# Cross-attention with a mixture of experts: transposes placed behind the bias, results read in five groups, scatters that leave out empty rows

## The chip, the cores and the metric

The kernel runs on one core of a Trainium2 chip. The metric is the device time of one execution in microseconds (us), the median of several runs. TensorE (PE in the profile, PEld its weight loads), VectorE (DVE), ScalarE (ACT), GpSimd (POOL) and SyncE (SP) run side by side and wait for one another by semaphores. SP, ACT and POOL issue the transfers (DMA).

## What is computed

All arrays are float32. `x` is (4, 512, 512), the context (4, 1024, 512).

```python
def attention(query, kv):                       # 16 heads of 32
    q, gate = query @ Wq.T, sigmoid(query @ Wg.T + bg)
    k, v = split(kv @ Wkv.T, 2)
    q, k = f(q), f(k)                           # f(x) = x + 1 if x > 0 else exp(x), per head
    z = 1 / (q . k.sum(tokens) + 1e-6)
    return (q @ (k.T @ v) * z * gate) @ Wo.T

def experts(x):                                 # 8 experts, each token goes to its best 2
    w, sel = top_k(x @ Wr, 2); w = softmax(w)
    return sum over the 2 choices of w * (x @ We[sel] + be[sel])

x = x + attention(layernorm(x), context)
x = x + experts(layernorm(x))
```

The two choices of a token are computed apart: 4 x 512 tokens make 4,096 rows that go through an expert.

## The kernel before

**Order of the work.** The four batches go through attention one after the other. After the attention of batch b, `choose` (L466) makes the normalized rows and picks two experts for each token, and `dispatch` (L514) works out by counting (small matmuls on ones) at which place of its expert's list each choice stands, and scatters the rows into `stream`, an array in DRAM with a region for each expert. A row carries two more numbers: where its result belongs (`home`), and its first expert.

**Expert tiles.** A tile is 128 rows of one expert's region. How many rows an expert has is known only on the chip, so lists of tiles are computed there: `tiles_of` (L582) counts tiles, `spans` (L593) orders them by groups and experts, `listed` (L614) writes for each tile the row at which it begins, and its expert. There are two lists. The early list (17 tiles, `EARLY`) is made when batch 3's attention is under way, from tiles that batches 0 to 2 have filled; it has three groups. The late list (up to 22 tiles, `LATE`; 18 of them, `SURE`, are always worked on, the rest stand behind a branch) is made after the dispatch of batch 3, from all that is left; its four groups are ordered so that the first tiles complete the results of batch 1, then 2, then the first half of 3, then the rest. Its wide operations on VectorE have 22 tiles x 4 groups x 8 experts = 704 columns.

**A step.** `run` (L671) is a generator that works through a list. For tile j, `rows` (L675) issues five loads on SP: four quarters of the rows, in 128-byte pieces, and a small one, `of`, with the two extra numbers. `turned` (L709) transposes the rows on VectorE in 32x32 blocks (L715) and computes the target row of each result from `of`: L724 makes `at` (home plus 1 if this is the token's second choice), L729 makes `to`, the smaller of `at` and `unread`. A row of `stream` without a token carries a home beyond every result; `unread` gives such a row a target of its own past the 4,096 results, so that it is written where nothing reads. `expert` (L735) does the matmuls with the expert's weights, adds the bias into `y` (L753) and lets GpSimd scatter `y` to the rows of `result` (L757). Step j loads tile j + 5, transposes tile j + 3, and then does the expert of tile j, whose bias is ordered behind that transpose; transposes and their small followers keep the order of the text. Early transposes go to four places in turn, so the transpose of tile j + 4 needs the matmuls of tile j to be done.

**Reading back.** The 16 token tiles (four a batch) each read their 256 rows of `result` (`fetch`, L810, 512 KB), add the two weighted results to the attention's output (`add`, L834, two VectorE operations), and store the tile (`store`, L849). `plan` and `begins` (L864 to L874) say at which step this is done: the reads of token tiles 0 to 3 at late steps -3 to 0 (negative steps are the last early ones), 4 to 7 at 5 to 8, 8 to 11 at 12 to 15, 12 and 13 at 16 and 17; adds three steps later, stores one after that. `also(j)` (L876) issues what is planned for step j, behind `y` of that step on VectorE and behind its scatter on GpSimd. What falls at step 18 or later comes after the loop, and there token tiles 14 and 15 are read by SP and ACT once all scatters have landed. A read waits for the scatters of as many tiles as `MOSTLY` says (13, 21, 29, 33 for the four batches). Whether that was enough is computed on the chip: `where_to_read` (L798) compares a group's last tile with the limit; if it was not, the read goes to rows of zeros at `NOWHERE`, and a branch at the end (L1020) reads everything again.

**Queues.** Scatters, reads and stores of the loop share GpSimd's queue, in the order of the text, each with a small memset (`mark`) ahead of it. SP issues the row loads. The order of the late list's instructions on VectorE among the steps is chosen when the program is built, mostly by the order of the text, and by when it is taken to be ready.

Of the kernel before, what the change touches and what calls it, by code (L numbers as in the profile page):

```python
# [9 lines left out]
F32 = mybir.dt.float32  # L10
I32 = mybir.dt.int32
# [6 lines left out]
P = 128  # L18
# [27 lines left out]
MOSTLY = (13, EARLY + 4, EARLY + 12, EARLY + 16)  # L46
NOWHERE = 2 * TOK + LATE * P
GROUPS = 4
# [3 lines left out]
def xattn_moe_kernel(  # L52
# [29 lines left out]

# [125 lines left out]
    unread = numbers("unread", [[P, LATE]], [P, LATE], base=2 * TOK, channel=1)  # L208
    expert_no = numbers("expert_no", [[0, GROUPS], [1, E]], [P, GROUPS, E])
    tile_no = numbers("tile_no", [[1, LATE]], [P, LATE])  # L210
# [303 lines left out]
    def dispatch(b):  # L514
# [21 lines left out]
        if b == B - 1:  # L536
            matmul(
                out=pp[:, NT + 1, :], lhsT=ones, rhs=acc[:, NT // 2, :], start=True, stop=True
            )
            counts["half"] = const.tile([P, E], F32, name="half")  # L540
            nc.vector.tensor_copy(counts["half"], pp[:, NT + 1, :])
# [72 lines left out]
    def listed(groups, n, name):  # L614
# [6 lines left out]
        def temp(what):  # L621
            t = work.tile([P, LATE * GROUPS * E], F32, tag="ex", name=what)
            return t[:, 0 : n * s].rearrange("p (n s) -> p n s", s=s)
# [47 lines left out]
    def run(lists, lo, n, early):  # L671
# [3 lines left out]
        def rows(j):  # L675


            row = nc.values_load(
                row_i[0:1, j : j + 1], [ET.SP], min_val=0, max_val=SLOTS,
                skip_runtime_bounds_check_because=why,  # L680
            )
            if j % 5 < 3:
                xg = cpool.tile([P, ROW], F32, tag="cT", name="xg")
            else:
                xg = kvpool.tile([P, ROW], F32, tag="v", name="xg", bufs=2)
            of = small.tile([P, 2], F32, tag="of", name="of", bufs=8)
            rows_of = stream[ds(row, P), :]
            parts = []
            for i in range(NC):
                parts.append(  # L690
                    (
                        xg[ts(i, HD), 0:D].rearrange("t (j f) -> t j f", j=NC),
                        rows_of[:, ts(i, P)].rearrange("(j t) f -> t j f", t=HD),
                    )
                )
            parts.append((of, rows_of[:, D:ROW]))
            for dst, src in parts:
                load = nc.sync.dma_start(out=dst, in_=src)  # L698
                latest["load"] = load
                if early:  # L700
                    behind(load, written["stream"][: 2 * NT * (B - 1)], "tokens of the tile")
                    early_loads.append(load)
                    for put in scatters.get(B - 1, []):
                        tc.declare_no_dep(load.ins, put.ins, reason=full_already)
                else:
                    behind(load, written["stream"], "tokens of the tile")
            return xg, of

        def turned(j, xg, of):  # L709
# [3 lines left out]
            else:  # L713
# [7 lines left out]
            at = small.tile([P, 1], F32, tag="at", name="at", bufs=8)  # L721
            tc.keep_in_program_order(latest["turn"])
            tc.keep_in_program_order(
                nc.vector.tensor_scalar(  # L724
                    at, of[:, 1:2], ranked[:, j : j + 1], of[:, 0:1],
                    ALU.is_equal, ALU.add,
                )
            )
            latest["turn"] = nc.vector.tensor_scalar(  # L729
                home_i, at, unread[:, j : j + 1], None, ALU.min  # L730
# [4 lines left out]
        def expert(j, xT, home_i):  # L735
# [15 lines left out]
            else:  # L751
# [9 lines left out]
                in_offset=None,  # L761
            )
            apart(put, "result", "each choice has a row; rows without a token go unread")
# [3 lines left out]

# [6 lines left out]
        def ahead(j):  # L774
            if j + 5 < n:
                with tc.issue_after(latest["load"].ins) if latest else nullcontext():
                    loaded.append(rows(j + 5))
            if j + 3 >= lo and loaded:
                ready.append(turned(j + 3, *loaded.pop(0)))

        for j in range(lo - 5, lo):
            ahead(j)
        yield
        for j in range(lo, n):
            ahead(j)
            with tc.issue_after(latest["turn"].ins):
                expert(j, *ready.pop(0))
            yield
# [3 lines left out]
    homes = [(wpool, "wq"), (wpool, "wg"), (wpool, "wo"), (big, "xT"), (big, "aT")]  # L792
    fetched = {}

    rows_of, spots = {}, {}
    soon = const.tile([P, B], F32, name="soon")

    def where_to_read(b, many, most):  # L798

        flag = soon[:, b : b + 1]  # L800
        nc.vector.tensor_scalar(flag, many, most, None, ALU.is_gt)
        spot = small.tile([P, 1], F32, tag="spot", name="spot")
        first_row = float(2 * L * b)
        nc.vector.tensor_scalar(
            spot, flag, float(NOWHERE) - first_row, first_row, ALU.mult, ALU.add
        )
        spots[b] = const.tile([P, 1], I32, name=f"spot_{b}")
        nc.vector.tensor_copy(spots[b], spot)

    def fetch(t, tiles, queue, sure=True):  # L810
# [5 lines left out]
        if sure:  # L816
            src = flat[:, t]
        else:
            b, o = t // NT, t % NT * 2 * P
            if b not in rows_of:  # L820
                rows_of[b] = nc.values_load(
                    spots[b][0:1, 0:1], [queue.engine], min_val=0, max_val=NOWHERE,
                    skip_runtime_bounds_check_because="one of two constants",
                )
            src = result[ds(rows_of[b] + o, 2 * P), :].rearrange("(p i) f -> p i f", i=2)
# [36 lines left out]
    half = B * NT - NT // 2  # L862
# [4 lines left out]
    begins = (-3, 5, 12, 16)  # L867
    for t in range(half):
        begin = begins[t // NT] + t % NT
        plan(begin, fetch, t, MOSTLY[t // NT], nc.gpsimd, False)  # L870
        step = begin + 3
        plan(step, add, t, gates if step < SURE else gates_end)
        step += 1
        plan(step, store, t, nc.gpsimd if step < SURE else nc.scalar)  # L874
# [11 lines left out]
    for b in range(B):  # L886
# [10 lines left out]
        if not more:  # L897
# [3 lines left out]
            held = [tiles_of(counts[i], f"held{i}") for i in range(B - 1)]  # L901
            ahead = [per_expert(f"ahead{i}") for i in range(3)]
# [4 lines left out]
            early_list = listed(early_groups, EARLY, "A")  # L907
# [9 lines left out]
            where_to_read(0, first_left, float(MOSTLY[0]))  # L917
# [6 lines left out]
            next(early)  # L924
# [33 lines left out]
    for j, _ in enumerate(early, 10 - EARLY):  # L958
        with tc.issue_after(latest["y"].ins):
            also(j)  # L960
# [10 lines left out]
    for count in (*held[1:], tiles_of(counts["half"], "held3"), tiles_of(counts[3], "held4")):  # L971
# [3 lines left out]
    late_list = listed(late_groups, LATE, "B")  # L975
    late_i = const.tile([P, 1], I32, name="late_i")
    nc.vector.tensor_copy(late_i, late_groups[2][:, GROUPS - 1, E - 1 : E])
    for g in range(GROUPS - 1):
        where_to_read(
            g + 1, late_groups[2][:, g, E - 1 : E], float(MOSTLY[g + 1] - EARLY)  # L980
        )
# [6 lines left out]
    next(late)  # L988
    for j, _ in enumerate(late):
# [78 lines left out]
```

## Time and profile before

Three runs took 623.1 to 625.0 us. The profiled execution took 627.28 us, of which the span from the first to the last instruction is 625.7.

| | us |
|---|---|
| median of the runs | 623.54 |
| profiled execution, its own time | 627.28 |
| span of the profile | 625.7 |
| first early expert matmul (PE) | 453.3 |
| late list: first counting operation, end of the row list (DVE) | 511.7, 525.0 |
| first load of a late tile (SP) | 525.8 |
| first and last late expert matmul (PE) | 533.4, 599.3 |
| last scatter of results (POOL) | 605.0 |
| last two reads of results (SP, ACT) | 610.4, 610.6 |
| last add ends (DVE) | 621.4 |

In the groups of the page, a line names the source line, the engine, the operation and the tiles (`out<-in`), then how many there were and their busy time. In the order of time, a line has the start, the duration, the engine, line and operation, and in brackets how long the engine was idle before it and what ended that. In this kernel a tile is best followed by its names: `xg` the loaded rows, `turned_rows` (early) and `xgT` (late) the transposed ones, `pe` the matmul's result, `y` both the expert's output and the rows that are read back.

### The profile page before, as it was taken

The numbers are of one execution on the slowest core, as the hardware profiler recorded it, in microseconds if no ns is written. First come the engines' busy times: TensorE is split into PE (matmuls) and PEld (weight loads), VectorE is DVE, ScalarE is ACT, GpSimd is POOL, SyncE is SP. The second block draws the span as 40 slices with busy tenths as digits, with TensorE's granted clock in tenths as the row PEclk, the third lists the DMA queues.
The fourth block names the chain that finished last, engine by engine and source line by source line (L and its number), as shares of the span: only waits on it lengthen the run. The fifth ranks groups of instructions, "written<-read, shape, count | busy, mean of one in ns | idle before, by whom it ended". The sixth has DMA issues, their size and how long they took to land. (4 is left out here: it accounts for less than half of the span.)

```text
span 625.7 us, 6552 instructions
## 1 busy us (share of the span) xinstructions
PE 589.5 (94%) x1906; PEld 286.0 (46%) x1906; DVE 275.9 (44%) x698; ACT 115.2 (18%) x180; POOL 101.8 (16%) x265
## 2 busy tenths in 40 slices
PE   7999999999999999999999999999999999999930
PEld 3555543454564345446643444564344554444310
DVE  1322243217216341351554126218765487575762
ACT  1322222112321211142222112321300200000000
POOL 4100000000003100000050000003111245544550
PEclk9999999999999999999999999999999999999985
DMA  8648930682586127528430560932354434879785
GB/s 310 186 164 300 278 93 2 169 238 70 163 246 191 67 86 235 152 84 242 162 136 1 202 203 19 376 123 108 95 117 124 118 119 165 241 229 268 228 295 192
DMA packets 68596, 106.32 MB, mean 170 GB/s; under 512 B 11792, under 2 KB 30224, under 8 KB 68176
## 3 DMA queue, kind: packets, MB, share of 16 engines
q1 hardware_dynamic: 58944, 76.24, 41.2%
q0 software_dynamic: 8176, 27.56, 12.5%
q10 hardware_dynamic: 1440, 2.10, 1.0%
q8 instruction: 16, 0.26, 0.2%
q14 instruction: 20, 0.16, 0.1%
HBM read 45.93 MB, written 59.94 MB: 169 GB/s over the span
## 5 line engine op out<-in xcount | busy, mean ns | idle before, releaser
L90 PE MATMUL pk<-wkv_sb,cT 128*128 128x512 f32 x256 | 118.9, 609 | 4.7 <-DMA cT<-in_cT_dram 4.7
L90 PE MATMUL pv<-wkv_sb,cT 128*128 128x512 f32 x256 | 115.2, 593 | 0.0
L216 DVE TENSOR_SCALAR ex<-pk 128x512 f32<-128x512 f32 x32 | 22.0, 688 | 149.0 <-PE pk L90 149.0
L90 PEld LDWEIGHTS pv<-wkv_sb,cT 128*128 128x128 f32 x256 | 48.4, 190 | 62.3 <-issue 59.3
L90 PEld LDWEIGHTS pk<-wkv_sb,cT 128*128 128x128 f32 x256 | 47.8, 195 | 58.4 <-issue 50.4
L90 PE MATMUL pe<-we_sb,xgT 128*128 x144 | 63.9, 598 | 2.1 <-DVE xgT L715 1.8
L90 PE MATMUL pe<-we_sb,turned_rows 128*128 x136 | 60.0, 596 | 0.0
L273 POOL MEMSET v<- 128x4 f32 x32 | 3.3, 105 | 345.7 <-PE kvs L90 282.7
L90 PE MATMUL pg<-xT,wg_sb 128*128 128x512 f32 x128 | 56.7, 595 | 0.0
L90 PE MATMUL pq<-xT,wq_sb 128*128 128x512 f32 x128 | 56.6, 596 | 0.0
L90 PE MATMUL po<-wo_sb,aT 128*128 128x512 f32 x128 | 55.6, 592 | 0.0
L217 ACT ACTIVATE ex<-ex 128x512 f32<-128x512 f32 x48 | 30.2, 630 | 137.0 <-DVE ex L216 127.1
L757 POOL DMA_INDIRECT result<-y,to x35 | 37.3, 1066 | 95.8 <-DVE y L753 92.6
L90 PEld LDWEIGHTS pe<-we_sb,xgT 128*128 128x128 f32 x144 | 26.7, 190 | 39.1 <-issue 30.1
L558 POOL DMA_INDIRECT stream<-row,slot x32 | 32.0, 1000 | 50.0 <-DVE cmp L586 22.8
L90 PEld LDWEIGHTS pe<-we_sb,turned_rows 128*128 128x128 f32 x136 | 25.4, 190 | 31.3 <-issue 29.4
L90 PEld LDWEIGHTS kvs<-v,k 128*128 128x128 f32 x256 | 33.3, 191 | 13.4 <-issue 13.4
L90 PEld LDWEIGHTS pg<-xT,wg_sb 128*128 128x128 f32 x128 | 24.0, 190 | 32.1 <-issue 32.1
L90 PEld LDWEIGHTS po<-wo_sb,aT 128*128 128x128 f32 x128 | 24.1, 190 | 29.2 <-issue 28.5
L90 PEld LDWEIGHTS pq<-xT,wq_sb 128*128 128x128 f32 x128 | 23.8, 190 | 27.3 <-issue 27.3
L90 PE MATMUL kvs<-v,k 128*128 128x129 f32 x256 | 34.0, 275 | 0.0
L753 DVE TENSOR_TENSOR y<-pe,be_sb 128x512 f32<-128x512 f32 x35 | 24.0, 689 | 20.0 <-PE pe L90 10.1
(169 smaller groups left out, 466.4 us busy)
## 6 DMA issues: line engine op xcount, KB each, us to landing
stream<-empty SPq DMA_DIRECT2D x24, 1028.0 KB, 9.3
stream<-empty SPq DMA_DIRECT2D x8, 1285.0 KB, 10.0
xg<-stream SPq DMA_DIRECT2D x140, 64.0 KB, 2.2
we_sb<-in_we_dram SPq DMA_DIRECT2D x32, 256.0 KB, 6.2
cT<-in_cT_dram SPq DMA_DIRECT2D x31, 256.0 KB, 3.0
y<-result POOLq DMA_DIRECT2D x14, 512.0 KB, 6.5
x<-in_x_dram SPq DMA_DIRECT2D x16, 256.0 KB, 7.6
out_dram<-y POOLq DMA_DIRECT2D x10, 256.0 KB, 3.7
```

The lines of the kernel that those rows point to most:

```text
L90: tc.keep_in_program_order(nc.tensor.matmul(**operands))
L216: nc.vector.tensor_scalar(ex, src, 0.0, None, ALU.min)
L217: nc.scalar.activation(ex, ex, AF.Exp)
L273: nc.gpsimd.memset(v[:, :, P : P + 1], 1.0)
L558: put = nc.gpsimd.indirect_dma_start(out=stream, out_offset=bass.IndirectOffsetOnAxis(ap=slots[i][:, t, :], axis=0), in_=rows[t], in_offse ...
L753: latest["y"] = nc.vector.tensor_tensor(y, pe, be_sb[:, ds(no, 1), :].rearrange("p o f -> p (o f)"), ALU.add)
L757: put = nc.gpsimd.indirect_dma_start(out=result, out_offset=bass.IndirectOffsetOnAxis(ap=home_i, axis=0), in_=y, in_offset=None,)
```

## The change

Five things are altered.

- In `run`, a step loads tile j + 5, does the expert of tile j, and then transposes tile j + 3, which is now ordered behind the bias of tile j on VectorE. The five steps ahead of the first expert yield one by one; those of the late list are interleaved with early steps 12 to 16. The making of the late list now stands in the text between early steps 11 and 12; it stood behind step 16.
- The target of a result is one operation: home plus 1 or 0, converted. A row without a token keeps its home beyond the end, and the scatter gets a bound (`bounds_check`) of the last result row, and skips rows past it. `unread` and the rows that it named are gone.
- Results are read in five groups (`READ`) instead of four: batch 2 is split into halves. For this, `dispatch` also counts half of batch 2 (one matmul of ones and a copy), `tiles_of` runs once more, ahead of the early list, and the late list has five groups and 22 x 5 x 8 = 880 columns.
- The plan of the reads: token tiles 8 and 9 at steps 10 and 11, 10 and 11 at 14 and 15 as before, 12 and 13 both at step 17. Tiles read at step 14 or later are added and stored after the loop, so 10 and 11 go there too. The limits are 13, 21, 26, 29 and 33 tiles.
- `where_to_read` works on all late groups at once. The late list's two wide temporaries live in the places of `wo` and `aT`; the places of the pairs of token tiles 6, 7 and 8, 9 are exchanged, and so is the place at which the late row buffers begin their turn.

```diff
-MOSTLY = (13, EARLY + 4, EARLY + 12, EARLY + 16)
-NOWHERE = 2 * TOK + LATE * P
-GROUPS = 4
+READ = (
+    (0, 4, 13), (4, 8, EARLY + 4), (8, 10, EARLY + 9), (10, 12, EARLY + 12), (12, 14, EARLY + 16)
+)
+NOWHERE = 2 * TOK
+GROUPS = len(READ)
...
-        if b == B - 1:
+        if b >= B - 2:
             matmul(
                 out=pp[:, NT + 1, :], lhsT=ones, rhs=acc[:, NT // 2, :], start=True, stop=True
             )
...
-            if j % 5 < 3:
+            if (j if early else j + EARLY) % 5 < 3:
...
-            tc.keep_in_program_order(
-                nc.vector.tensor_scalar(
-                    at, of[:, 1:2], ranked[:, j : j + 1], of[:, 0:1],
-                    ALU.is_equal, ALU.add,
-                )
-            )
             latest["turn"] = nc.vector.tensor_scalar(
-                home_i, at, unread[:, j : j + 1], None, ALU.min
+                home_i, of[:, 1:2], ranked[:, j : j + 1], of[:, 0:1],
+                ALU.is_equal, ALU.add,
             )
...
-            )
-            apart(put, "result", "each choice has a row; rows without a token go unread")
+                bounds_check=2 * TOK - 1,
+                oob_is_err=False,
+            )
+            apart(put, "result", "each choice has a row")
...
-        def ahead(j):
-            if j + 5 < n:
-                with tc.issue_after(latest["load"].ins) if latest else nullcontext():
-                    loaded.append(rows(j + 5))
-            if j + 3 >= lo and loaded:
-                ready.append(turned(j + 3, *loaded.pop(0)))
-
-        for j in range(lo - 5, lo):
-            ahead(j)
-        yield
-        for j in range(lo, n):
-            ahead(j)
-            with tc.issue_after(latest["turn"].ins):
-                expert(j, *ready.pop(0))
+        def after(what):
+            return tc.issue_after(latest[what].ins) if what in latest else nullcontext()
+
+        for j in range(lo - 5, n):
+            if j + 5 < n:
+                with after("load"):
+                    loaded.append(rows(j + 5))
+            if j >= lo:
+                with after("turn"):
+                    expert(j, *ready.pop(0))
+            if j + 3 >= lo and loaded:
+                with after("y"):
+                    ready.append(turned(j + 3, *loaded.pop(0)))
             yield
...
-    homes = [(wpool, "wq"), (wpool, "wg"), (wpool, "wo"), (big, "xT"), (big, "aT")]
+    homes = [(wpool, "wq"), (wpool, "wg"), (wpool, "wo"), (big, "aT"), (big, "xT")]
...
-    begins = (-3, 5, 12, 16)
-    for t in range(half):
-        begin = begins[t // NT] + t % NT
-        plan(begin, fetch, t, MOSTLY[t // NT], nc.gpsimd, False)
-        step = begin + 3
+    begins = (-3, -2, -1, 0, 5, 6, 7, 8, 10, 11, 14, 15, SURE - 1, SURE - 1)
+    for g, (lo, hi, most) in enumerate(READ):
+        for t in range(lo, hi):
+            plan(begins[t], fetch, t, most, nc.gpsimd, g)
+    for t, begin in enumerate(begins):
+        step = begin + (3 if begin < SURE - 4 else SURE)
         plan(step, add, t, gates if step < SURE else gates_end)
-        step += 1
-        plan(step, store, t, nc.gpsimd if step < SURE else nc.scalar)
+        plan(step + 1, store, t, nc.gpsimd if step + 1 < SURE else nc.scalar)
...
+            held_half = tiles_of(counts[B - 2.5], "held_half")
...
     dispatch(B - 1)
-    for j, _ in enumerate(early, 10 - EARLY):
-        with tc.issue_after(latest["y"].ins):
-            also(j)
+    for _ in range(2):
+        next(early)
...
     late = run(late_list, 0, SURE, False)
-    next(late)
-    for j, _ in enumerate(late):
+    for j in range(-5, SURE):
+        if j < 0:
+            next(early)
+        next(late)
         with tc.issue_after(latest["y"].ins):
             also(j)
```

## The prediction

> **What bounds the kernel now.** I read the page's busy times first, then the busy times by stretch, then the order of time on VectorE and GpSimd, last the chain that ended last.
>
> ```profile
> PE 589.5 (94%) x1906; PEld 286.0 (46%) x1906; DVE 275.9 (44%) x698; ACT 115.2 (18%) x180; POOL 101.8 (16%) x265
> ```
> ```profile
> core 0: us, PE busy (x) PEld busy (x) DVE busy (x) ACT busy (x) POOL busy (x), PEclk, DMA share, GB/s
> ...
> 555.00:577.00 22.00, 21.13 (x48) 8.95 (x48) 13.41 (x29) 0.00 (x0) 10.76 (x25) 1.00 0.87 251
> 577.00:600.00 23.00, 21.67 (x48) 8.79 (x48) 16.52 (x34) 0.00 (x0) 13.39 (x32) 1.00 0.81 242
> 600.00:612.00 12.00, 0.00 (x0) 0.00 (x0) 6.63 (x12) 0.00 (x0) 5.73 (x19) 0.70 0.83 294
> 612.00:626.00 14.00, 0.00 (x0) 0.00 (x0) 4.35 (x6) 0.00 (x0) 0.00 (x0) 0.50 0.54 179
> ```
> TensorE is the bound until 599.3 us: an expert tile is eight matmul records of 0.434 us, 3.47 us, and the first 94% of the span has hardly a gap. The 18 late tiles begin at 533.36 and end at 599.34, 65.98 us where 18 x 3.47 = 62.5 would do, so some 3.4 us are lost there. Then 26.4 us follow without a matmul, and it is here that the change works. VectorE's order of time shows why TensorE begins late tile 12 at 577.17 and the next three at 581.0, 584.83 and 588.77, 3.87 apart instead of 3.47:
>
> ```profile
> 573.55 0.27 DVE L724 TENSOR_SCALAR at<-of,rankedB 128x1 f32<-128x1 f32 x1 [1.48 <-DMA of<-stream]
> ...
> 574.36 0.69 DVE L753 TENSOR_TENSOR y<-pe,be_sb 128x512 f32<-128x512 f32 x1 [0.29 <-issue]
> 574.97 0.74 DVE L840 SCALAR_TENSOR_TENSOR y<-y,gates,x 128x512 f32<-128x512 f32 x1
> 575.75 0.75 DVE L840 SCALAR_TENSOR_TENSOR y<-y,gates 128x512 f32<-128x512 f32 x1
> 576.41 0.70 DVE L715 STREAM_TRANSPOSE xgT<-xg 128x512 f32<-128x512 f32 x1
> ```
> The transpose of tile 12 stands behind y of tile 8, and that y stands behind the transpose of tile 11 and its `at`, which waited for a load. From there a step with an add costs VectorE 3.87 us, and TensorE follows. At the end:
>
> ```profile
> 597.86 0.75 DVE L840 SCALAR_TENSOR_TENSOR y<-y,gates,x 128x512 f32<-128x512 f32 x1 [2.18 <-DMA y<-result]
> ...
> 599.32 0.68 DVE L753 TENSOR_TENSOR y<-pe,be_sb 128x512 f32<-128x512 f32 x1
> 601.03 0.75 DVE L840 SCALAR_TENSOR_TENSOR y<-y,gates,x 128x512 f32<-128x512 f32 x1 [1.02 <-DMA y<-result]
> ...
> 602.48 0.68 DVE L753 TENSOR_TENSOR y<-pe,be_sb 128x512 f32<-128x512 f32 x1
> ```
> ```profile
> 604.16 0.53 POOL L827 DMA_DIRECT2D y<-result  x1 [2.20 <-issue]
> ...
> 605.00 1.51 POOL L757 DMA_INDIRECT result<-y,to  x1 [0.23 <-issue]
> ```
> ```profile
> 610.39 7.96 DMA y<-result
> 618.45 0.76 DVE y L840
> ```
> The last y (tile 17) begins 3.1 us after its last matmul, because the adds of token tiles 8 and 9 stand ahead of it and wait for their reads. Its scatter then sits on GpSimd behind the read of token tile 12 (step 16), which waits for the scatter of late tile 15 to land. The reads of token tiles 14 and 15 go out when that scatter has landed, 610.39, land at 618.4, and adds and stores end the span at 625.7.
>
> **Part 1, one instruction less per tile.** L724 and L729 become one of the same shape as L724 (0.23 us): 0.21 and some 0.05 of issue gone, so a step with adds falls from 3.87 to about 3.6 us. Worth 4 x 0.27 = 1.1 us in the stretch from 573 to 589, nothing where VectorE idles.
>
> **Part 2, transpose j+3 behind y of j.** The instructions stay; y no longer waits for a later tile's load. In the stretch shown, y of tile 8 (its matmuls ended at 565.7) comes ahead of the wait that ended at 573.55, which takes 0.69 and 0.5 of issue from in front of transpose 12. Against it, each transpose loses the lead of half a step. Lead left: y of j comes 0.7 us after tile j ends, transpose j+3 takes 0.7, and tile j+3 starts 6.94 us after tile j ends, about 5.5 us. Where VectorE is filled with the late list (511.7 to 525.6) the lead is less: y of early tile 12 stood at 525.76 and early tile 15 was due at 526.6, so its transpose behind that y ends near 527.3, a stall of 0.7 us. I take it as made good later, by the 3.4 us of gaps in which TensorE waits for loads that SP issues on a clock of its own; without that cover it costs 0.7.
>
> **Part 3, five groups.** One more counting matmul in `dispatch` of batch 2: six such records took 0.81 us, a matmul is two, +0.27 us on a full TensorE. `held_half` adds two operations of 0.29 on VectorE ahead of the early list, whose first transpose (451.45) ended 1.1 us before TensorE needed it: hidden. The late list's five wide operations grow from 704 to 880 columns, 0.88 to some 1.1 us each, four of them ahead of the row list: +0.9, and 0.5 for one group more in `spans`; one early transpose with its two followers (1.1) leaves that stretch. The row list, ready at 524.99, comes at about 525.3. SP's first late load waits for it and for the token scatters, the last of which was issued at 520.96. Cover: TensorE still has early tiles 14 to 16 until 533.4.
>
> **Part 4, reads moved.** Token tiles 8 and 9 are read at steps 10 and 11 instead of 12 and 13 (512 KB each, median landing 6.5 us). y of tile 10 came at 582.02, so the reads leave at about 583 and 586.5 instead of 592.58 and 594.51, and land near 590 and 593; their adds, now in steps 13 and 14, hardly wait, and nothing stands ahead of y 16 and 17. What is late next is the add of tile 9 at about 594, ahead of y 15, with 3 us in hand. The read of 12 moves from step 16 to 17, behind the last scatter. The adds of 10 and 11 now lie with those of 12 to 15 after the loop (1.5 us each). I counted the routing of the reference's inputs: the four late groups are full after 4, 9, 10 and 15 late tiles, their limits are 4, 9, 12 and 16, so no group is read again.
>
> **Part 5, skipped rows.** 35 scatters of 128 rows for 4,096 choices: 384 rows, 0.79 MB at 2 KB, no longer written, nearly all by late tiles. At the last 105 us' mean of 233 GB/s that is 3.4 us of transfer time, spread over stretches 81 to 89% full; I count none on the path. What the bound check costs GpSimd no row shows: from nothing (the present 0.97 to 1.24 us) to a third rival below. I take nothing, since the nearest row, L558 with the same 128 rows, has 0.97.
>
> **Sum**, against the span of 625.7. The last matmul ends at 598.3 instead of 599.3 (-1.1 -0.7, of which late loads give back half, +0.27: -1.0, from -2.5 to +2). The last y begins 0.3 after it instead of 3.1: -2.8 (0 to -2.8). Its scatter follows 1.8 after y's start, with tile 16's ahead of it, instead of 2.52: -0.7. So it leaves at 600.5 instead of 605.0, lands 5.0 later as before, and the closing reads leave at about 605.9. They took 8.0 with token tile 13's read and stores beside them; now 12 and 13 leave at 602.6, some 300 GB/s moves nine tenths of a megabyte by 605.9, and what is left beside them is as much as before: 8.0 (7 to 11). The adds of 12 and 13 may stand in the way of 14's: +0.3 (0 to 3). In all -4.2: span 621.5. The runs' median is 623.54, 2.2 below the profiled span (its own run 627.28); I apply the difference: **619.3 us**, own range 617 to 621.5.
>
> On the closing reads, the Trainium skill, DMA: Bandwidth & Descriptors, section Anatomy of one DMA, fits a transfer by 2.0 us plus its bytes over 436 KB a microsecond. For 1 MB that is an estimate of 4.4 us against the 8.0 here, and the sum would give about 615.7; the trace's rows decide.
>
> **Rivals.** (1) The reads moved to 583 and 586.5 meet the loads of late tiles 15 to 17, issued from 579.60 to 588.98. Such loads land in 2.2 us as a median of the run and 4.0 in the last 105 us; late tile 5's was transposed 9.1 us after its issue began, with four reads beside it. Were tile 17's so late, its transpose would begin at 595.7, its matmuls end at 600.0, and scatter and all follow 2 us later: 621.3. For it: 81% full already. Against: 3 us of lead. Chance 0.16. The Trainium skill (DMA: Bandwidth & Descriptors, section Issuing engines are not separate DMA queues) has the rule: whichever engine starts them, the transfers share sixteen DMA engines and interleave, and 6.91 us for late tile 4's last part beside the reads agrees.
>
> (2) The bias costs more: the late list, ahead of early steps 12 to 16 in the text now, is also put ahead of y 10. The list's own work is 8.5 us (13.3 less two steps), 1.3 more now, so y 10 falls to 521.5 and transpose 13, behind it, ends at 522.9 where tile 13 is due at 519.6: 3.3 us of TensorE idle. Not made good later: 622.6, no change by measurement. For it: VectorE 19.2 of 24 us busy there. Against: in the present order y 10 stands in the middle of the list. Chance 0.16.
>
> (3) The other side: the bound check makes the scatter long and GpSimd the bound. A step with read and store costs GpSimd the scatter s plus 0.57, 0.58, two marks and gaps, s + 1.6; it passes 3.47 from s = 1.9. At s = 3.0 the four steps with both lose 1.1 each and some six with one 0.5 each, 7.4 us: 626.7. It makes the kernel slower than before from about s = 2.7. For it: this scatter alone changes its form. Against: 0.97 now, and rows left out are descriptors saved. Chance 0.18.
>
> (4) The skip does nothing, the bytes stay: no time in my sum hangs on it, so it is inside the forecast, as 0.79 MB more.
>
> **Chances.** Forecast 0.50; rivals 0.16, 0.16, 0.18. What counts as a change is 0.3%, 1.9 us: below 621.7 or above 625.4. Faster: 0.49 of the forecast, 0.11 and 0.05 of the first two rivals, 0.65. Same: 0.01, 0.05, 0.10 and 0.01, 0.17. Slower: 0.18. The range 616.0 to 625.5 leaves out 0.02 below and 0.16 above.
>
> **What would show it.** Right: the last L753 within 1 us of the last matmul, the last scatter near 600.5, no 3.87 us steps, the closing reads near 606, GpSimd's written rows down by 384. Wrong: an idle TensorE of over 1.5 us between 515 and 533 (rival 2), waits for xg after 585 (rival 1), L757 over 1.9 us (rival 3), or closing adds that wait in a row, which would leave the gain at 2 to 3 us.

## The result and the profile after

The changed kernel takes **621.87 us** (median of 20 runs, 619.56 to 624.12). The kernel before took 625.04 us on the same chip (20 runs, 622.39 to 628.31). The ratio is 0.9948, with an interval from 0.9934 to 0.9962: faster, by 3.2 us of the medians. One execution differs from the next by some 2 us either way, in every kernel of this study, so a single profile shows a mechanism but not the size of a small gain. The profiled execution of the changed kernel took 622.61 us, its span 621.0 (before 627.28 and 625.7).

The page of the changed kernel: busy times, the DMA total, GpSimd's DMA queue, and the group of the result scatters.

```profile
PE 588.5 (95%) x1908; PEld 286.3 (46%) x1908; DVE 271.0 (44%) x668; ACT 115.2 (19%) x180; POOL 100.6 (16%) x274
...
DMA packets 68597, 105.55 MB, mean 170 GB/s; under 512 B 11981, under 2 KB 30413, under 8 KB 68176
...
q0 software_dynamic: 8176, 26.78, 12.1%
...
L757 POOL DMA_INDIRECT result<-y,to x35 | 35.8, 1023 | 93.7 <-DVE y L753 88.4
```
VectorE has 30 instructions less. GpSimd's queue moves 26.78 MB instead of 27.56, which is the 384 skipped rows, and a scatter takes 1,023 ns as a mean (1,066 before): the bound check adds nothing that this shows.

TensorE's order of time, with the start, the duration and, in brackets, the idle time ahead and what ended it:

```profile
526.93 7.13 PE L91 MATMUL pe<-we_sb,turned_rows 128*128 x16 [0.75 <-DVE turned_rows L721]
533.91 31.06 PE L91 MATMUL pe<-we_sb,xgT 128*128 x72
565.20 3.70 PE L91 MATMUL pe<-we_sb,xgT 128*128 x8 [0.23 <-DVE xgT L721]
569.28 28.03 PE L91 MATMUL pe<-we_sb,xgT 128*128 x64 [0.38 <-DVE xgT L721]
```
The stall of 0.75 us ahead of early tile 15 is there. From 569.28 on, eight late tiles follow without a gap, where the kernel before had four steps of 3.87 us. The late tiles end at 597.31 and take 63.4 us instead of 65.97. (A second profile of the same kernel, under e5 below, has 66.0, so this profile alone doesn't show a gain there.)

VectorE's order of time at the end, and GpSimd's:

```profile
594.62 1.52 DVE L753 TENSOR_TENSOR y<-pe,be_sb 128x512 f32<-128x512 f32 x2
597.35 0.69 DVE L753 TENSOR_TENSOR y<-pe,be_sb 128x512 f32<-128x512 f32 x1 [1.21 <-PE pe L91]
...
606.92 0.75 DVE L840 SCALAR_TENSOR_TENSOR y<-y,gates_end 128x512 f32<-128x512 f32 x1
614.13 0.75 DVE L840 SCALAR_TENSOR_TENSOR y<-y,gates_end,x 128x512 f32<-128x512 f32 x1 [6.45 <-DMA y<-result]
```
```profile
598.18 1.02 POOL L757 DMA_INDIRECT result<-y,to  x1 [0.27 <-DVEq L1012]
...
600.06 0.56 POOL L827 DMA_DIRECT2D y<-result  x1 [0.64 <-issue]
...
600.71 0.55 POOL L827 DMA_DIRECT2D y<-result  x1
604.72 1.03 POOL L757 DMA_INDIRECT result<-y,to  x1 [3.46 <-issue]
```
The last y begins at once when the last matmul ends. Its scatter doesn't: on GpSimd it stands behind the reads of token tiles 12 and 13 (600.06, 600.71) and behind the branch that skips the spare tiles (L1012). On that branch the engine's sequencer spends 2.00 us, from 601.50, on an increment of a DMA semaphore for the skipped block. So the scatter leaves 7.4 us after the last matmul.

The reason is in how the order is written. `keep_in_program_order` ties an instruction to the one before it on its engine. At the first read of each group a register load (L820), which nothing ties down, stands between the step's scatter and the read's mark, and the chain breaks there. In this profile the first reads of all five groups (steps -3, 5, 10, 14 and 17) leave ahead of their own step's scatter; no other read does but that of token tile 13, which is tied to the read of 12. The kernel before has two such reads, at steps -3 and 5, and they cost nothing. This is step 5, the read of token tile 4 and then that step's scatter, on GpSimd in the kernel before:

```profile
563.45 0.57 POOL L827 DMA_DIRECT2D y<-result  x1 [0.69 <-PE pe L90]
...
564.32 1.02 POOL L757 DMA_INDIRECT result<-y,to  x1 [0.23 <-DVE to L729]
```
The read at 604.16 ahead of the last scatter is none of them: the text puts the read of step 16 ahead of the scatter of step 17. Now the break falls on step 17, and both reads and the branch pass ahead of the last scatter.

The chain that ended last, its final steps:

```profile
604.72 2.33 DMA result<-y,to
607.30 6.38 DMA y<-result
614.91 1.43 DVE y L840 x2
```
The late scatter lands in 2.3 us instead of 4.3, and the closing reads take 6.4 us instead of 8.0. In the kernel before, these reads didn't wait for that landing last. The scatter had landed at 609.33, and the reads, on SP and ACT, also wait for semaphores that the skipped block's increment raises. There it stands behind the scatter, in the listing of the branch's line by engine:

```profile
L1003 POOLq INC_SWDGE_SEM  x1: 2022/2022/2022, 608.1 to 608.1; - x1
```
It ends at 610.10, and the reads leave at 610.39. So the increment ended the wait before the change; in the changed kernel it is over early, and delays the scatter instead.

The busy times by stretch fit the shorter landings:

```profile
core 0: us, PE busy (x) PEld busy (x) DVE busy (x) ACT busy (x) POOL busy (x), PEclk, DMA share, GB/s
...
577.00:600.00 23.00, 20.32 (x47) 8.31 (x45) 14.96 (x27) 0.00 (x0) 11.94 (x28) 1.00 0.80 244
600.00:612.00 12.00, 0.00 (x0) 0.00 (x0) 5.54 (x8) 0.00 (x0) 2.92 (x12) 0.51 0.69 207
```
From 600 to 612 the DMA engines are 69% busy at 207 GB/s, where they were 83% busy at 294: while the last scatter waited, other transfers came to their end.

### The profile page after: what moved, and what is told of

Same layout as the page of the kernel before. It is cut to its first block, busy times and chain, and to the rows that moved or that the text cites. A ratio compares the mean times of both kernels' runs of the same rounds, so it can differ in the third digit from the quotient of the medians.

```text
span 621.0 us, 6578 instructions
## 1 busy us (share of the span) xinstructions
PE 588.5 (95%) x1908; PEld 286.3 (46%) x1908; DVE 271.0 (44%) x668; ACT 115.2 (19%) x180; POOL 100.6 (16%) x274
## 3 DMA queue, kind: packets, MB, share of 16 engines
q0 software_dynamic: 8176, 26.78, 12.1%
## 5 line engine op out<-in xcount | busy, mean ns | idle before, releaser
L757 POOL DMA_INDIRECT result<-y,to x35 | 35.8, 1023 | 93.7 <-DVE y L753 88.4
L223 DVE SCALAR_TENSOR_TENSOR k<-pk,ex 128x512 f32<-128x512 f32 x32 | 22.1, 690 | 19.5 <-ACT ex L222 19.5
```

What stands on the lines that cost most here:

```text
L223: nc.vector.scalar_tensor_tensor(dst, src, 0.0, ex, ALU.max, ALU.add)
L757: put = nc.gpsimd.indirect_dma_start(out=result, out_offset=bass.IndirectOffsetOnAxis(ap=home_i, axis=0), in_=y, in_offset=None, bounds_ch ...
```

## The experiments

Twelve runs were made, in three groups (e5 is the changed kernel once more, e9 is e8). Within a group all ran on one chip, with shared runs of the kernel before.

| run | what it is | median us (runs) | before | ratio and interval |
|---|---|---|---|---|
| e1 | change, reads pinned behind scatters | 621.99 (12) | 624.91 | 0.9965 [0.9943, 0.9987] |
| e2 | change, transposes first | 623.87 (12) | 624.91 | 0.9983 [0.9963, 1.0002] |
| e3 | change, old read plan | 621.29 (11) | 624.91 | 0.9942 [0.9918, 0.9966] |
| e4 | kernel before, skip alone | 622.55 (12) | 624.91 | 0.9963 [0.9938, 0.9988] |
| e5 | change, unaltered | 623.07 (12) | 625.9 | 0.9968 [0.9948, 0.9988] |
| e6 | change, no skip | 624.04 (12) | 625.9 | 0.9982 [0.9963, 1.0001] |
| e7 | change, early list first | 621.81 (12) | 625.9 | 0.9942 [0.9922, 0.9963] |
| e8 | e7 with e1 | 620.36 (6) | 625.9 | 0.9918 [0.9887, 0.995] |
| e9 | e8 again, as base | 619.17 (10) | 624.43 | 0.9918 [0.9893, 0.9944] |
| e10 | base, no skip | 623.51 (12) | 624.43 | 1.0 [0.997, 1.0029] |
| e11 | base, old read plan | 619.34 (9) | 624.43 | 0.9916 [0.9888, 0.9945] |
| e12 | base, transposes first | 622.0 (12) | 624.43 | 0.9954 [0.9932, 0.9976] |

### The last scatter kept ahead of the reads (e1)

```diff
             tc.keep_in_program_order(put)
+            latest["put"] = put
...
-        with tc.issue_after(latest["y"].ins):
+        with tc.issue_after(latest["y"].ins), tc.issue_after(latest["put"].ins):
             also(j)
```


> The changed kernel, with the reads and stores of a step ordered behind that step's scatter on GpSimd. In the changed kernel the last scatter left at 604.72, behind the reads of token tiles 12 and 13 and behind the branch. Theory A (that wait costs the end): the last scatter leaves near 598.5, lands near 602, the closing reads leave at 602 to 603 instead of 607.3 and take 8 instead of 6.4 with 12 and 13 beside them; 2 to 3 us less than the changed kernel, ratio to before 0.990 to 0.992. Theory B (the end is bound by the transfers): the closing reads take 9 us or more, ratio 0.994 to 0.996 as without the edit.

Measured: the order is as meant. The last scatter leaves at 601.68, 2.0 us after the last y, and the closing reads follow at 607.8. But the median is 621.99 us, ratio 0.9965, no better than the change itself (0.9948 and 0.9968 in its two groups). In its profile TensorE idles 1.31 us ahead of early tile 0, which neither the kernel before nor the first profile of the changed kernel shows. The gain of the pin was not seen here, and a new loss was. The closing reads left when the branch's increment ended (605.48 to 607.50), not when the scatter had landed (606.02): theory A's 602 to 603 leaves the increment out. Nor did the reads take theory B's 9 us: it was 4.2 us on SP and 5.9 us on ACT.

### The transposes first again (e2)

```diff
+            if j + 3 >= lo and loaded:
+                ready.append(turned(j + 3, *loaded.pop(0)))
             if j >= lo:
                 with after("turn"):
                     expert(j, *ready.pop(0))
-            if j + 3 >= lo and loaded:
-                with after("y"):
-                    ready.append(turned(j + 3, *loaded.pop(0)))
```


> The changed kernel, with the transpose of tile j + 3 ahead of the bias of tile j again. Theory A (the order lets TensorE lose less): the late tiles lose 2 to 3.4 us again instead of 0.9, the last matmul ends 1.5 to 2.5 later, and of that 1 to 2 us reach the end: ratio 0.997 to 0.999. Theory B (the order does not reach the end, since the last scatter waits behind reads and branch): ratio 0.994 to 0.996.

Measured: 623.87 us, ratio 0.9983. The gain is mostly gone, but the interval begins where that of the change ends (0.9962) and overlaps that of e5 (0.9948 to 0.9988), so this run alone didn't settle it; e12 does.

### The old plan of the reads (e3)

```diff
-    begins = (-3, -2, -1, 0, 5, 6, 7, 8, 10, 11, 14, 15, SURE - 1, SURE - 1)
+    begins = (-3, -2, -1, 0, 5, 6, 7, 8, 12, 13, 14, 15, 16, 17)
...
-        step = begin + (3 if begin < SURE - 4 else SURE)
+        step = begin + 3
```


> The changed kernel, with token tiles 8 and 9 read at steps 12 and 13 and tiles 12 and 13 at 16 and 17, adds three steps after the read, as before. Theory A (the moved reads free VectorE's queue ahead of the last biases): the last bias begins 2 to 3 us after its matmul again, the last scatter near 603 to 605 and the closing reads near 609: ratio 0.998 to 1.000. Theory B (the gain is that of the transposes): ratio 0.994 to 0.996.

Measured: 621.29 us, ratio 0.9942: with the reads of token tiles 8, 9, 12 and 13 back at their old steps, and the adds three steps behind their reads, the kernel is as quick as with them moved. This goes against the prediction, which put 2.8 us on the reads. The profiled execution, at 626.24 the slowest of the eleven, does show theory A's sign: its last y begins 1.8 us after the last matmul, with an add of 1.5 us just ahead of it. So the old plan can still put adds in the way; e11 tests it again.

### The skip alone, in the kernel before (e4)

```diff
-NOWHERE = 2 * TOK + LATE * P
+NOWHERE = 2 * TOK
-    unread = numbers("unread", [[P, LATE]], [P, LATE], base=2 * TOK, channel=1)
+    unread = numbers("unread", [[0, LATE]], [P, LATE], base=4 * SLOTS)
...
+                bounds_check=2 * TOK - 1,
+                oob_is_err=False,
```
The second instruction for the target stays; its minimum now changes nothing.

> The kernel before with the skipped rows alone: two operations for the target as before, the second now leaves it as it is, and the bound in the scatter. 0.78 MB less moved. Theory A (no time hangs on it): ratio 0.998 to 1.000. Theory B (the skip carries the gain): 0.994 to 0.996. A costly check on GpSimd: the scatter's mean over 1.2 us and a ratio above 1.002.

Measured: 622.55 us, ratio 0.9963, a gain of 2.4 us for four lines that touch no order. TensorE's order of time in this run:

```profile
532.03 41.36 PE L90 MATMUL pe<-we_sb,xgT 128*128 x96
573.82 7.54 PE L90 MATMUL pe<-we_sb,xgT 128*128 x16 [0.43 <-DVE xgT L715]
581.59 14.34 PE L90 MATMUL pe<-we_sb,xgT 128*128 x32 [0.24 <-DVE xgT L715]
```
The first twelve late tiles have no gap, where the kernel before had two; the steps of 3.8 to 4.0 us after them (tiles 11 to 14 begin at 569.8, 573.8, 577.7 and 581.6) are still there. This fits a skip that lets loads arrive sooner and leaves the VectorE-bound steps as they were, but one profile doesn't show it: the late tiles take 63.9 us here, and the two profiles of the changed kernel have 63.4 and 66.0.

### Is the gap ahead of early tile 0 the kernel's or the execution's (e5)

The changed kernel, unaltered.

> The changed kernel, unaltered, on the chip of the next three runs. Its earlier profile had no idle TensorE ahead of early tile 0, three of its variants had 1.9 to 2.2 us there. If that gap belongs to the execution and not to the kernel (theory G), this profile may show it as well: a bias-free check of pd's add on VectorE (L384) at about 442.3 instead of 440.6 and early tile 0 at about 454.5. If it belongs to the variants' edits, early tile 0 is again near 452.8. The median should be 621.9, ratio 0.995, by either.

Measured: 623.07 us, ratio 0.9968. This second profile has the gap. First line VectorE's, then TensorE's order of time:

```profile
440.76 0.69 DVE L384 TENSOR_SCALAR z<-pd 128x512 f32<-128x512 f32 x1 [1.26 <-remote]
```
```profile
452.75 3.70 PE L91 MATMUL pe<-we_sb,turned_rows 128*128 x8 [1.06 <-DMA xg<-stream]
...
584.16 15.70 PE L91 MATMUL pe<-we_sb,xgT 128*128 x32 [2.00 <-DVE xgT L721]
```
VectorE waits 1.26 us for the attention's denominators `pd` in the middle of the early row list, the list is late by as much, and TensorE waits for the first early rows. The gap belongs to the execution, as theory G has it. The times that were to show this did not come: L384 and early tile 0 stand where the first profile has them, because this execution was 1.2 us ahead until then (the matmuls of `pd` begin at 438.04 instead of 439.22). The profiles of e1, e2, e3 and e6 have the wait for `pd` as well (1.25 to 1.38 us, with gaps of 1.3 to 1.6 us on TensorE rather than 1.9 to 2.2); of this order of instructions only the first profile of the changed kernel has it not. What delays that completion the trace doesn't name ("remote"). The same profile shows 2 us lost ahead of late tile 14, whose rows landed late; such gaps fall elsewhere in each profile. With it the late tiles take 66.0 us, as long as before the change.

### The change without the skip (e6)

`NOWHERE`, `unread` and the two-step target as before the change, no bound on the scatter.

> The change without its last part: rows without a token are again written to rows past the tokens' results, with the second target instruction that this takes, everything else as in the changed kernel. Theory S (the skipped bytes make most of the gain): ratio 0.998 to 1.001, closing reads of 8 us and a landing of the last scatter of 4 to 5 us, 27.56 MB on GpSimd's queue. Theory R (order and moved reads make it): ratio at most 0.996.

Measured: 624.04 us, ratio 0.9982, against 623.07 for e5 beside it. The difference of 1.0 us lies within the intervals, so in the changed kernel itself the worth of the skip isn't settled; neither theory is ruled out here. The ratio is the one that theory S put, but its signs at the end did not come: the last scatter landed in 2.8 us, and the closing reads took 6.2 and 6.4 us.

### The early list ahead of the reciprocals (e7), and with the pin (e8)

```diff
-        z = inverses(qTs)
+        pd = inverses(qTs)
+        if more:
+            z = inverted(pd)
...
             where_to_read(slice(0, 1), first_left)
+            with tc.issue_after(scatters["A"].ins):
+                z = inverted(pd)
```
`inverted` holds the two VectorE instructions on `pd` (L384, L385), and `scatters["A"]` is the last copy of the early row list.

> The changed kernel with the reciprocal chain of the last half batch's attention (L384, L385: 4 us of VectorE) issued behind the early row list instead of in the middle of it. Theory G (the five groups use up the early list's margin, and some executions lose 1 to 2 us ahead of early tile 0): the list comes about 3.5 us earlier, no gap ahead of early tile 0 in the profile, 0.5 to 1.5 us less than the unaltered kernel in the median. Rival: the gap is the execution's and covered later, no difference beyond 0.5 us. Other side: z is now late for TensorE (pz at 450.7), and the gap moves there.

Measured: 621.81 us, ratio 0.9942, 1.26 us below e5 on the same chip. VectorE and TensorE in this run:

```profile
444.18 0.17 DVE L677 CAST rowiA<-rowA 128x17 int32<-128x17 f32 x1
444.25 0.68 DVE L387 TENSOR_SCALAR z<-pd 128x512 f32<-128x512 f32 x1
```
```profile
451.12 1.14 PE L91 MATMUL pz<-z,spread 32*128 32x512 f32 x8
...
453.21 3.70 PE L91 MATMUL pe<-we_sb,turned_rows 128*128 x8
```
The list is done at 444.35 (446.43 in e5), z is still in time for `pz`, and the gap is gone.

> The same with each read of results also pinned behind the scatter before it on GpSimd, so that the last scatter can't fall behind the reads of token tiles 12 and 13 and the branch. If the two things hid each other's gain, 619 to 620 (ratio 0.991 to 0.993), last scatter within 4 us of the last matmul. If the landing and closing reads only lengthen as the scatter gets earlier, because the transfers, not the order, set the end (theory T), the median stays within 0.5 us of the run with the list alone, and closing reads take 7.5 to 8 us instead of 6.4.

Measured: 620.36 us (six runs), ratio 0.9918; 1.45 us below e7. GpSimd's order of time and the end of the chain:

```profile
600.46 1.01 POOL L760 DMA_INDIRECT result<-y,to  x1 [0.23 <-DVE y L844]
...
601.50 0.59 POOL L831 DMA_DIRECT2D y<-result  x1
```
```profile
601.50 4.58 DMA y<-result
606.25 4.24 DMA y<-result
611.74 1.43 DVE y L844 x2
```
The scatter now leaves 2.0 us after the last matmul, ahead of the reads and 4.3 us earlier than in the change. It lands in 4.3 us instead of 2.3, at 604.78, so part of theory T holds: the earlier scatter, with other transfers beside it, lands slower. But the closing reads leave only at 606.25, 1.0 us earlier than in the change, and what they waited for last is no transfer. The increment at the branch stands behind the scatter again:

```profile
L1020 POOLq INC_SWDGE_SEM  x1: 2017/2017/2017, 603.9 to 603.9; - x1
```
It ends at 605.96. In all nine profiles that have it behind the last scatter (the kernel before, e1, e3, e4 and e8 to e12) the closing reads leave 0.29 us after its end, and 1.1 to 1.8 us after the scatter has landed.

The read on SP, which this chain shows, took 4.2 us, the one on ACT 5.8; in e9, the same kernel, both took 6.4. That part belongs to the execution. The median fell by 1.45 us, so the order was worth something.

This also goes some way to explain e1. Without the pin (the change, e5, e7) the closing reads leave at 607.2 to 607.4, whether the last matmul ends at 597.3, 599.9 or 598.5: reads, increment and scatter follow one another on GpSimd, and the last y has no say. With the pin (e1, e8, e9) they leave 7.8 to 8.2 us behind the last matmul. In e1 that ended at 599.64, late by the gap ahead of early tile 0, and nothing was won; in e8 it ended at 598.45. So the pin pays once the late tiles end early. These are single profiles; no run takes the branch and its increment away.

### Each part undone in the better version (e9 to e12)

e9 is e8 again.

> The early list ahead of the reciprocals and the reads pinned behind their scatters, as in the run before, now as the base of the next three on one chip, each of which undoes one part of the change in it. Ratio 0.990 to 0.994 again; no idle TensorE ahead of early tile 0, last scatter within 4 us of the last matmul.

Measured: 619.17 us, ratio 0.9918 [0.9893, 0.9944], as e8. No gap ahead of early tile 0; last matmul 598.49, last scatter 600.93.

e10 has e6's edit in it.

> The base with rows without a token written again. With the end now set by transfers behind an early last scatter, theory S expects 2 to 3 us more than the base (0.8 MB at some 260 GB/s is 3 us), in a longer landing of the last scatter and longer closing reads; theory R (the order makes the gain) at most 1 us more, as between the two runs without the pins (624.0 against 623.1).

Measured: 623.51 us (619.51 to 626.83), ratio 1.0: 4.3 us more than the base (2 to 3 were expected), and no gain is left. Theory S holds. Its profiled execution was one of the quick ones (621.20 us), so it can't show all of this, but the stretch behind the last matmul shows what fills it. This is the stretch in e10, then in e9:

```profile
600.00:612.00 12.00, 0.00 (x0) 0.00 (x0) 4.88 (x7) 0.00 (x0) 3.18 (x13) 0.60 0.92 315
```
```profile
600.00:612.00 12.00, 0.00 (x0) 0.00 (x0) 5.92 (x8) 0.00 (x0) 3.97 (x15) 0.66 0.82 257
```
Without the skip the DMA engines are 92% busy there at 315 GB/s, with it 82% at 257. e10 also brings back the second instruction for the target, which by the prediction's estimate costs 0.27 us in a step with adds; e4 keeps that instruction and still gains 2.4 us.

e11 has e3's edit in it.

> The base with token tiles 8, 9, 12 and 13 read at steps 12, 13, 16 and 17 and added three steps later, as before the change. By the prediction's step (reads at 592 to 594 put adds that wait ahead of the last y: 2.8 us) the last y stands 2 to 3 us behind the last matmul again and the run is 2 to 3 us longer than the base. By the rival, that adds wait only while GpSimd's queue is itself held up and the moved reads are worth nothing, within 0.7 us of the base, the last y within 0.6 us of the last matmul.

Measured: 619.34 us, ratio 0.9916, the same as the base: the rival holds, and the prediction's step on the reads falls (each of the two intervals is some 1.7 us wide to either side). The last y begins 0.7 us after the last matmul, near the rival's 0.6 and not the 2 to 3 us of the prediction's step. GpSimd's order of time:

```profile
583.26 0.98 POOL L760 DMA_INDIRECT result<-y,to  x1 [1.15 <-DVE y L756]
...
584.49 0.58 POOL L831 DMA_DIRECT2D y<-result  x1 [0.15 <-issue]
```
The read of token tile 8, at the very step it had before the change, leaves at 584.49 instead of 592.58. The scatter of late tile 12, behind which it stands, leaves at 583.26 instead of 590.72: y of that tile no longer lags by two to three tiles.

e12 has e2's edit in it.

> The base with each transpose ahead of the bias of three tiles before again, as before the change. If y waiting behind transposes that wait for loads is what lost TensorE 3.4 us in the late tiles, the late tiles take 1 to 3 us longer than in the base (64 to 65 us there) and the run 1 to 2 us; if the late tiles' gaps come from loads that are late by themselves, no difference beyond 0.5 us.

Measured: 622.0 us, ratio 0.9954, 2.8 us more than the base. The late tiles take only 0.8 us longer (65.4 against 64.6), less than expected; two profiles of one kernel differ by more. The order of the late steps shows another loss. VectorE's order of time in e12, then in e9, around the last two transposes:

```profile
594.11 0.71 DVE L724 STREAM_TRANSPOSE xgT<-xg 128x512 f32<-128x512 f32 x1 [1.55 <-SPq L1019]
...
595.16 0.69 DVE L756 TENSOR_TENSOR y<-pe,be_sb 128x512 f32<-128x512 f32 x1 [0.19 <-issue]
```
```profile
593.25 0.68 DVE L756 TENSOR_TENSOR y<-pe,be_sb 128x512 f32<-128x512 f32 x1
593.85 0.70 DVE L724 STREAM_TRANSPOSE xgT<-xg 128x512 f32<-128x512 f32 x1
```
In e12 the transpose of tile 17 waits for its rows until 594.11, with y of tile 14 behind it; in e9 that y has gone 1.9 us earlier. Its scatter, the reads behind it and the last scatter (602.85 against 600.93) are 1.9 to 2.2 us later in e12, and the closing reads 2.4 us (609.07 against 606.66). The two profiled executions lie only 0.8 us apart, 622.03 for e9 and 622.86, both on the slow side of their runs: they show the path, and the 2.8 us are the medians'.

## Why the prediction was right, and where not

The forecast of faster by 4.2 us, 619.3 of a range to 625.5, stands against 3.2 us and 621.87, which its own narrower range of 617 to 621.5 misses by 0.4. Of the 2.6 us between 619.3 and 621.87, 1.5 are the base, 623.54 in the three runs at hand then and 625.04 in twenty. The total is right partly by luck: errors cancel. In the profiled execution, with its span of 621.0 against the predicted 621.5:

- **Last matmul** at 598.3: 597.31 in the first profile, 599.86 in the second, inside the bounds of -2.5 to +2. The 3.87 us steps are gone, as worked out. Part 1 or part 2 by itself seems enough for that: they are gone in e6 (both target operations, new order) and in e12 (one operation, old order), and stand in e4 (both operations, old order). The waits for rows go on and move about (0.9 and 3.5 us lost over the late tiles).
- **Last y** 0.3 us after it: 0.04. The size is right, the reason in part 4 is not. The step "the reads leave at about 583 and 586.5 ... their adds hardly wait, and nothing stands ahead of y 16 and 17" came out even earlier (575.63 and 582.50), and the adds did not wait; but e3 and e11 put the reads back and show no loss. It was enough that y went ahead of the transposes and bytes fell away: in e11, which has both, the read of token tile 8 leaves 8 us sooner at its old step. With the skip alone (e4) it leaves at 589.1.
- **Last scatter** "leaves at 600.5": failed, 604.72. This is the step that was wrong. Its order on GpSimd was taken from the text of the kernel; the chain of pins breaks at the first read of a group, and the profile of before had shown it, with the read of step 5 at 563.45 ahead of its scatter at 564.32.
- **Landing 5.0, closing reads 8.0, adds +0.3**: 2.5 to the closing reads, 6.4, nothing. These durations were carried over as constants, but they depend on what else is under way. The 5.0 was no landing, either: the reading that the closing reads "go out when that scatter has landed" missed that it had landed after 4.3 us, and that the increment at the branch, which ended at 610.10, released them. Together: the closing reads left 1.4 us later than predicted, took 1.6 less, and the adds 0.3 less, -0.5 in all, which is the difference of the spans. The fit of the Trainium skill (DMA: Bandwidth & Descriptors, section Anatomy of one DMA) gave an estimate of 4.4 us for this megabyte; the page has it for single transfers that GpSimd issues, and these two are issued by SP and ACT. From the first issue to the last landing they took 6.4 us in the change and 6.0 in e8, the least of all profiles, so no run here agrees with it.
- **Part 2's stall** of 0.7 us ahead of early tile 15: 0.75. Late tiles began 0.55 us later than before and made it good. What part 2 is worth was sized too low: I counted one y out of the way of transpose 12 (0.7); e12 gives 2.8 us of the medians, and its profile shows a way, through scatters and reads behind each y.
- **Part 3's** `held_half` "hidden": in five of the six profiles of this order of instructions it isn't. The margin of 1.1 us is 0.96 in the first profile (the transpose ends at 451.84, early tile 0 begins at 452.80), and in e5 a completion that came 1.3 us late uses it up. The early list first gives back 1.3 us (e7).
- **Part 5**, "I count none on the path": mis-sized. The skip alone is worth 2.4 us (e4) and 4.3 us in the version with the early list first and the pin, with one instruction more per tile in that figure (e10); in the change itself 1.0, within the intervals (e6). An estimate from the packets: 195 of 4,096 bytes less, at 190 ns each, are 37 us of one DMA engine or 2.3 us of all sixteen, in a stretch in which these are 80 to 92% busy.

The rivals: (2), the list put ahead of y 10, did not come; TensorE's gap there is the 0.75. (3), a slow bound check, did not come (1,023 ns); its counter-argument, "rows left out are descriptors saved", isn't borne out either, as the last section shows. (4), a skip that does nothing, is refuted by the bytes (26.78 MB for 27.56). Of (1), late loads, the second profile has a case (2.0 us ahead of tile 14), but e11, whose reads leave later, is no quicker, so that the moved reads cause such gaps isn't shown.

What stays open: what delays the completion of `pd`, what the end would be without the increment at the branch, and how the skip's gain splits between earlier loads and a shorter end. Parts 1 and 3 were not undone by themselves.

The version that beats both kernels is the base: 619.17 us, 5.3 us below the kernel before (ratio 0.9918).

## What to carry to other kernels

- Bytes that nobody reads cost time where the DMA engines are nearly full, even if no transfer of them is on the chain that ended last. Here 0.78 MB cost 2.4 us (e4) and 4.3 us (e10) in a stretch 80 to 92% busy; look for such bytes before reordering reads.
- On an in-order engine, what waits for a transfer should stand behind what is ready (here y ahead of the transpose). What it delays can show up queues further on, in scatters and reads, and not on the engine itself.
- Check the issue order of each DMA queue in the trace rather than in the text, and don't carry a landing time over to a schedule in which it starts beside other transfers. Look at what an engine really waited for: here the increment for a skipped block held the closing reads.

## What the hardware showed that was not expected

A skipped row is not absent from the queue. Its transfer shrinks to 4 bytes: GpSimd's queue has 8,176 packets before and after, with 195 of the 4,672 of 4,096 bytes turned into 189 of 8 bytes (two skipped rows each) and 6 of 2,052; an 8-byte one takes 8 to 9 ns instead of some 190 as a mean. And a block of GpSimd DMAs that a branch skips still costs that engine 2.00 to 2.02 us in every profile, for the semaphores that its DMAs would have raised (`INC_SWDGE_SEM`). Whoever waits for these semaphores waits for it too: the closing reads in nine of the fourteen profiles.
